# Rows of h_prime by VectorE transposes and DMA hops instead of TensorE, with layer 0 begun three steps sooner

## The chip, the cores and the metric

The kernel runs on one core of a Trainium2 chip. A core has a matrix engine (TensorE, "PE" in the profile), a vector engine (VectorE, "DVE"), an activation engine (ScalarE, "ACT"), a general engine (GpSimd, "POOL") and SyncE ("SP"), which here only issues DMA transfers. Each engine works through its own list of instructions in order; between engines there are semaphores. The metric is the time on the device in microseconds, the median of the runs.

## The reference: what is computed

There are 16 samples, each a graph of 1024 nodes with 128 features and a 1024x1024 adjacency matrix of zeros and ones. Two layers follow one another; each is wrapped in a residual sum and a layer normalization over the features.

```
# layer 0
h = x Ww^T + Wb
e = (h A) h^T;  e = e + e^T
attention = softmax(where(adj > 0, e, 0), axis=1) * adj
h_prime = relu(attention h)
ic = sigmoid(h_prime wi_u + x wi_x)      # one number per node; fc and oc alike
out0 = oc * tanh(ic * h_prime + fc * x)
x = layernorm(x + out0)
# layer 1, four heads
h = x conv_w[hd] + conv_b[hd]
Ah = tanh(adj * (h attn_w[hd] h^T))
Xm = relu(mean over heads of relu(Ah h))
x = layernorm(x + relu(Xm + x))
```

The three gates ic, fc and oc need, for each node, a dot product of its row of h_prime with a vector of 128 weights.

## The kernel before

All is float32. A sample's 1024 nodes are eight blocks of 128 (`NB = 8`), and 1024 columns are two halves of 512 (`NH = 2`).

**The order of work** is written out by hand. The main loop (L602 to L625) goes over samples `b`, and for each over 32 steps of layer 1: four heads times eight blocks `m`. A step (`layer1_step`, L477) is: two score matmuls into PSUM tiles of the tag "sc" (L494), two VectorE products with the adjacency tile (L495), one tanh on ScalarE (L496), and then the `back` of the step two before (`DELAY = 2`), four matmul instructions into `acc` (L500). A float32 matmul of 512 columns shows as two instructions in the profile. On a head's last block `back` also adds the head to the sample's sum on VectorE (L516, L518); with the delay that falls into steps 9, 17, 25 and into step 1 of the next sample. `acc` of layer 1 has a single buffer, so a head's first `back` comes after the sum of the head before. There are four "sc" buffers, used in turn by nearly all PSUM results except the two accumulators.

**Layer 0 of the next sample** is cut into pieces with short names, and the list `BETWEEN` (L592) says which pieces follow which step of layer 1; `AHEAD` (L598) does so for the sample after that. The pieces: L loads xT and the eight adjacency tiles, X loads x; Q and H project; S0 to S7 compute the scores of one row of blocks (upper triangle only); T0 to T6 mirror a row of blocks into the lower triangle; A masks, takes the maximum and exponentiates; B multiplies with the adjacency, scales, and issues the `back` of the block before into `acc0` (L351); R applies relu and leaves h_prime transposed in `hpT` (features in partitions). P and p then bring h_prime into rows: eight TensorE matmuls with `hpT` as the weights against `ident_g` (L370), which is the identity with the three gate vectors as further columns, so the same matmul gives h_prime's rows and its three dot products; ScalarE copies them out (L371). G forms the gates (L377 to L380) and fc * x on GpSimd (L384). I, O, V, N form the inner sum and tanh, the outer sum, the statistics, and the normalized result x1.

**Turning by VectorE and DMA.** `turn` (L220) transposes a 128x1024 tile without TensorE: VectorE transposes each 32x32 block (L224), SyncE writes the tile to DRAM (L226), waits until it has landed, and reads it back by four DMAs with the blocks moved to their places (L229). It is used for x1 (`turn_x1`, after step `TURN`) and for the sum of heads (`layer1_end`, whose four parts come after the steps of `ENDING`); `turn_score` (T, L312 to L319) does the same for the scores. All these DMAs, and the loads, are issued by SyncE, whose queue is in order: while it waits for a write to land, what is behind it waits too.

Layer 0 of sample 0 and the beginning of sample 1's are written out before the loop (L561 to L588), with TensorE doing the transposes of sample 0.

Of the kernel before, what the change touches and what calls it, by code (L numbers as in the profile page):

```python
# [11 lines left out]
F32 = mybir.dt.float32  # L12
AF = mybir.ActivationFunctionType
ALU = mybir.AluOpType
# [3 lines left out]
P = 128  # L18
# [4 lines left out]
def two_layer_adjacency_kernel(  # L23
# [41 lines left out]
    mhalf = consts.tile([P, NB], F32, name="mhalf")  # L65
    nc.gpsimd.memset(mhalf, -0.5)

    a_in = consts.tile([P, P], F32, name="a_in")
    nc.sync.dma_start(a_in, A)
    ww_in = consts.tile([P, P], F32, name="ww_in")  # L70
    nc.sync.dma_start(ww_in, Ww)
    wb_col = consts.tile([P, 1], F32, name="wb_col")
    nc.sync.dma_start(wb_col, Wb.rearrange("(d o) -> d o", o=1))
# [13 lines left out]
    for t, ws in ((gate_x, (wi_x, wf_x, wo_x)), (gate_u, (wi_u, wf_u, wo_u))):  # L87
        for g, w in enumerate(ws):
            nc.scalar.dma_start(t[:, g : g + 1], w.rearrange("(d o) -> d o", o=1))

    def load_late_weights():
        nc.sync.dma_start(cw_in[0:1], conv_b.rearrange("(o h) d -> o h d", o=1))
        nc.sync.dma_start(cw_in[1:P], conv_w[:, 0 : D - 1, :].rearrange("h f d -> f h d"))
        nc.sync.dma_start(cw_last, conv_w[:, D - 1 : D, :].rearrange("h f d -> f h d"))
        nc.sync.dma_start(aw, attn_w.rearrange("h i j -> i h j"))

# [12 lines left out]

    a_sym = consts.tile([P, P], F32, name="a_sym")
    s_ww = consts.tile([P, P], F32, name="s_ww")
    q_w = consts.tile([P, P], F32, name="q_w")
    c_col = consts.tile([P, 1], F32, name="c_col")
    sb_col = consts.tile([P, 1], F32, name="sb_col")
# [101 lines left out]
    def turn(dst, src, name):  # L220


        t = sb.tile([P, N], F32, tag="turn", name=f"turn_{name}", bufs=2)
        nc.vector.transpose(t.rearrange("p (k d) -> p k d", d=P), src)  # L224
        d = dram.tile([P, N], F32, tag="turn", name=f"dram_{name}")
        nc.sync.dma_start(d, t)  # L226
        dv = d.rearrange("(a i) (k c j) -> c i k a j", i=Q, c=P // Q, j=Q)
        for c in range(P // Q):
            nc.sync.dma_start(  # L229
                dst[ts(c, Q)].rearrange("i (k a j) -> i k a j", a=P // Q, j=Q), dv[c]  # L230
            )
# [4 lines left out]
    def layer0(b):  # L236
# [4 lines left out]

        t = {}

        def load():
            t["xT"] = sb.tile([P, N], F32, tag="xT", name=f"xT_{b}")
            nc.sync.dma_start(t["xT"], xT[b])
            adj_t[b] = []
            for j in range(NB):
                a = adjp.tile([P, N], F32, tag="adj", name=f"adj_{b}_{j}")
                nc.sync.dma_start(a, adjT[b, ts(j, P), :])  # L250
                adj_t[b].append(a)

        def load_x():
            t["x"] = sb.tile([P, NB, D], F32, tag="x", name=f"x_{b}", bufs=1)
# [68 lines left out]

        def mask(j):
            s = t["R"][:, :, j, :]
            adj = adj_t[b][j].rearrange("p (k d) -> p k d", d=P)
            for ks in (ts(0, BH), ts(1, BH)) if (b, j) == (0, 0) else [slice(NB)]:
                nc.vector.scalar_tensor_tensor(  # L328
                    s[:, ks], adj[:, ks], 0.0, s[:, ks], op0=ALU.is_gt, op1=ALU.mult
                )  # L330
            nmax = sb.tile([P, 1], F32, tag="nmax", name=f"nmax_{b}_{j}", bufs=4)
            nc.vector.tensor_reduce(nmax, s, AX.XY, ALU.max, negate=True)  # L332
            t["z", j] = sb.tile([P, 1], F32, tag="z", name=f"z_{b}_{j}", bufs=4)
            nc.scalar.activation(s, s, AF.Exp, bias=nmax, accum_out=t["z", j])  # L334

        def weigh(j):

            s = t["R"][:, :, j, :]
            nc.vector.tensor_mul(s, s, adj_t[b][j].rearrange("p (k d) -> p k d", d=P))  # L339
            rz = sb.tile([P, 1], F32, tag="rz", name=f"rz_{b}_{j}", bufs=4)  # L340
            nc.vector.reciprocal(rz, t["z", j])  # L341
            t["hz", j] = sb.tile([P, D], F32, tag="hz", name=f"hz_{b}_{j}", bufs=4)
            nc.scalar.mul(t["hz", j], t["h"][:, j, :D], rz)  # L343
            if j:
                back(j - 1)
# [16 lines left out]
        def rows_hp(groups):  # L362

            if groups[0] is GROUPS[0]:
                t["hp"] = sb.tile([P, NB, D + 3], F32, tag="hp", name=f"hp_{b}", bufs=1)
            for ks in groups:
                pt = small(f"pt0_{b}_{ks[0]}")[:, : len(ks) * (D + 3)]
                pt = pt.rearrange("p (k d) -> p k d", d=D + 3)
                for i, k in enumerate(ks):
                    nc.tensor.matmul(pt[:, i, :], t["hpT"][:, ts(k, P)], ident_g, start=True, stop=True)  # L370
                nc.scalar.copy(t["hp"][:, ks[0] : ks[-1] + 1, :], pt)  # L371

        def gates():

            gate = t["gate"]
            gflat = gate.rearrange("p k g -> p (k g)")
            nc.vector.tensor_add(gate, t["hp"][:, :, D : D + 3], gate)  # L377
            nc.scalar.activation(gflat, gflat, AF.Exp, scale=-1.0)
            nc.vector.tensor_scalar_add(gflat, gflat, 1.0)
            nc.vector.reciprocal(gflat, gflat)  # L380
            t["u"] = sb.tile([P, NB, D], F32, tag="u", name=f"u0_{b}", bufs=1)
            t["x1"] = sb.tile([P, NB, D + 1], F32, tag="x1", name=f"x1_{b}")
            for ks in PARTS:
                nc.gpsimd.tensor_mul(  # L384
                    t["u"][:, ks], t["x"][:, ks],
                    gate[:, ks, 1:2].to_broadcast([P, ks.stop - ks.start, D]),
                )
            nc.gpsimd.memset(t["x1"][:, :, 0:1], 1.0)

        def inner(halves):  # L390
            u, gate, hp = t["u"], t["gate"], t["hp"]
# [19 lines left out]
        def finish(p):  # L411
# [4 lines left out]

        PARTS = [slice(0, NB)] if b else [slice(0, BH), slice(BH, NB)]
        pieces = {
            "L": load, "X": load_x, "R": relu,
            "P": lambda: rows_hp(GROUPS[:-1]), "p": lambda: rows_hp(GROUPS[-1:]),  # L420
            "G": gates,
        }
        for i, ks in enumerate(GROUPS):
            pieces[f"H{i}"] = partial(project_h, [ks])
        for p in range(len(PARTS)):
# [4 lines left out]
        for q in range(NH):  # L430
            pieces[f"Q{q}"] = partial(project_q, q)
        for j in range(NB):
            for name, piece in (("S", score), ("A", mask), ("B", weigh)):
                pieces[f"{name}{j}"] = partial(piece, j)
            if j + 1 < NB:
                pieces[f"T{j}"] = partial(turn_score, j)
        return pieces

    def run(pieces, names):
        for name in names.split():  # L440
            if name in pieces:
                pieces.pop(name)()
# [33 lines left out]

    def layer1_step(b, hd, m):  # L477
        x1T, h1, uT = x1T_t[b], h1_t[b, m], u_t[b, hd]
        adj = adj_t[b][m]
        if m == 0:  # L480
            acc1_t[b, hd] = ps_acc.tile([P, N], F32, tag="acc1", name=f"acc1_{b}_{hd}")
        acc = acc1_t[b, hd]


        last = (b, hd) == (B - 1, H - 1)
        if last:
            if m == 0:
                kept.append(sb.tile([P, NB, N], F32, tag="R", name="kept", bufs=1))
            s = kept[0][:, m, :]
        else:  # L490
            s = sb.tile([P, N], F32, tag="s1", name=f"s1_{b}_{hd}_{m}", bufs=4)
        for q in range(NH):
            ps = ps_sc.tile([P, 512], F32, tag="sc", name=f"sc1_{b}_{hd}_{m}_{q}")
            nc.tensor.matmul(ps, x1T[:, ts(m, P)], uT[:, ts(q, 512)], start=True, stop=True)  # L494
            nc.vector.tensor_mul(s[:, ts(q, 512)], ps, adj[:, ts(q, 512)])  # L495
        nc.scalar.activation(s, s, AF.Tanh)  # L496

        def back(halves=range(NH)):
            for q in halves:
                nc.tensor.matmul(  # L500
                    acc[:, ts(q, 512)], h1[:, ts(hd, D)], s[:, ts(q, 512)],
                    start=(m == 0), stop=(m == NB - 1),
                )
            if m == NB - 1:
                if hd == 0:
                    sum_t[b] = sb.tile([P, N], F32, tag="sum", name=f"sum_{b}", bufs=1)
                for q in halves:
                    add_head(b, hd, acc[:, ts(q, 512)], q * 512)

        push(partial(back, [0]) if last else back)  # L510
# [31 lines left out]
    def last_end(b, k0, k1):  # L542
# [16 lines left out]


    first, second, join = layer0(0), layer0(1), join_weights()  # L561
    run(first, "L X")
    load_late_weights()
    run(second, "L")
    run(first, "Q0 H0 S0 H1 H2 Q1 T0 S1 A0 T1 S2 A1 B0 T2 S3 A2 B1 T3 S4 A3 B2 T4 S5 A4 B3")
    run(first, "T5 S6 A5 B4 T6 S7 A6 B5")
    run(second, "Q0")
    run(first, "A7 B6")
    run(second, "Q1")
    run(first, "B7 R")  # L570
    next(join)
    run(first, "P p G")
    run(second, "H0 H1")
    next(join)
    run(second, "S0")
# [14 lines left out]


    BETWEEN = [  # L592
# [4 lines left out]
    ]  # L597
    AHEAD = {28: "L", 31: "Q0 Q1"}  # L598
    TURN = 27
    ENDING = (DELAY, DELAY + 3, DELAY + 5, DELAY + 7)  # L600
    end, nxt = None, second
    for b in range(B):  # L602
        after = layer0(b + 2) if b + 2 < B else {}
# [72 lines left out]
```

## Time and profile before

Median of 3 runs 2452.89 us (2452.03 to 2454.49). The profiled execution spans 2453.0 us.

| engine | busy us | share |
|---|---|---|
| TensorE, matmuls | 2428.0 | 99% |
| VectorE | 1590.2 | 65% |
| ScalarE | 1082.8 | 44% |
| GpSimd | 112.9 | 5% |

| group | instructions | busy us | mean ns |
|---|---|---|---|
| L370 TensorE, h_prime's rows and gate products | 256 | 33.8 | 275 |
| L371 ScalarE, their copies of 393 and 262 columns | 32 and 16 | 15.6 and 6.0 | 487 and 377 |
| L224 VectorE, block transposes of 128x1024, each of two uses | 15 | 18.5 | 1235 |
| L332 VectorE, a reduction of 128x1024 | 128 | 156.2 | 1220 |
| L384 GpSimd, a product of 128x1024 | 15 | 28.5 | 1898 |

In a line of groups, the first part is line, engine, operation, written and read tiles and shapes; then the count, busy time and mean duration; then the idle time of the engine just ahead of these instructions and what ended it. A line of a timeline is start, duration, engine, line, operation. Matmul instructions overlap in the records (592 ns each, while one starts every 429 ns), so TensorE's pace is read from starts.

### The profile page before, as it was taken

To read this page: it belongs to the slowest core of one execution; us is meant where nothing else is said; L and a number is where in the kernel's file an instruction comes from. 1 tells how busy PE (TensorE), PEld (TensorE's weight loads), DVE (VectorE), ACT (ScalarE), POOL (GpSimd) and SP (SyncE) were. 2 spreads that over 40 slices of the span, in tenths; PEclk is the share of its full clock that TensorE was granted. 3 is DMA by queue.
4 is the path that set the end of the run, shared out by engine and by line. 5 is a ranking of instruction groups with operands and counts; after the bars stand their busy time and mean duration, and the time that the engine had idled before them with its cause. 6 is when DMAs were issued, how large, how long until landed. Compare 5 with 4: busy or idle time off the path is not lost.

```text
span 2453.0 us, 19886 instructions
## 1 busy us (share of the span) xinstructions
PE 2428.0 (99%) x6175; PEld 1121.2 (46%) x6175; DVE 1590.2 (65%) x3017; ACT 1082.8 (44%) x1522; POOL 112.9 (5%) x94
## 2 busy tenths in 40 slices
PE   8999999999999999999999999999999999999998
PEld 4444444444444444444444444444444444444444
DVE  6665847657476575865658666585765857658454
ACT  5444444444444444434444444444444444444432
POOL 0000000000000000000000000000000000000000
PEclk9999999999999999999999999999999999999999
DMA  4204223041240512405123140332404223042010
GB/s 174 58 11 133 56 94 86 9 145 44 95 95 3 152 35 94 95 15 147 27 104 85 41 129 20 119 70 76 102 12 130 60 94 84 11 135 55 17 26 9
DMA packets 409056, 180.76 MB, mean 74 GB/s; under 512 B 352630, under 2 KB 377078, under 8 KB 408951
## 3 DMA queue, kind: packets, MB, share of 16 engines
q1 hardware_dynamic: 405927, 171.63, 25.1%
q0 software_dynamic: 2160, 7.87, 1.1%
q8 instruction: 49, 0.80, 0.1%
q14 instruction: 56, 0.46, 0.1%
q10 hardware_dynamic: 864, 0.00, 0.0%
HBM read 127.80 MB, written 51.64 MB: 73 GB/s over the span
## 4 chain that ended last, share of the span: by engine, by line
PE 92%; DVE 3%; DMA 2%; SPq 1%; POOL 0%; issue 0%; ACT 0%; POOLq 0%; DVEq 0%; ACTq 0%
PE sc L494 33%; PE acc L500 33%; PE acc L351 9%; PE sc L287 5%; PE pT_u L200 4%; PE pR L465 4%; DMA xT<-in_xT_dram 2%; PE pT_q L200 1%; PE pt L370 1%; PE pR_h L271 1%; SPq L229 1%; DMA dram_x<-turn_x 1%; DVE x L191 0%; DVE st L183 0%; POOL rs L188 0%
## 5 line engine op out<-in xcount | busy, mean ns | idle before, releaser
L495 DVE TENSOR_TENSOR s<-sc,adj 128x512 f32<-128x512 f32 x1008 | 671.3, 685 | 625.6 <-PE sc L494 613.8
L494 PE MATMUL sc<-uT,x1T 128*128 128x512 f32 x2048 | 962.0, 592 | 0.0
L500 PE MATMUL acc<-s,h 128*128 128x512 f32 x2016 | 947.4, 592 | 0.0
L496 ACT ACTIVATE s<-s 128x1024 f32<-128x1024 f32 x504 | 532.9, 1057 | 806.0 <-DVE s L495 799.6
L500 PEld LDWEIGHTS acc<-s,h 128*128 128x128 f32 x2016 | 381.7, 190 | 483.7 <-issue 474.4
L494 PEld LDWEIGHTS sc<-uT,x1T 128*128 128x128 f32 x2048 | 385.7, 190 | 468.8 <-issue 421.9
L351 PE MATMUL acc<-R,hz 128*128 128x512 f32 x512 | 241.2, 594 | 4.8 <-ACT hz L343 4.8
L334 ACT ACTIVATE R<-R,nmax 128x1024 f32<-128x1024 f32 x128 | 147.0, 1148 | 210.4 <-DVE nmax L332 182.4
L339 DVE TENSOR_TENSOR R<-R,adj 128x1024 f32<-128x1024 f32 x128 | 156.2, 1220 | 5.4 <-ACT R L334 0.2
L332 DVE TENSOR_REDUCE nmax<-R 128x1 f32<-128x1024 f32 x128 | 156.2, 1220 | 4.4
L328 DVE SCALAR_TENSOR_TENSOR R<-adj,R 128x1024 f32<-128x1024 f32 (+1 forms) x129 | 153.2, 1188 | 1.4 <-PE turn L305 1.4
L351 PEld LDWEIGHTS acc<-R,hz 128*128 128x128 f32 x512 | 95.6, 190 | 111.7 <-issue 85.6
L287 PE MATMUL sc<-xT,qT 128*128 128x512 f32 (+3 forms) x384 | 145.8, 489 | 0.5 <-ACT R L290 0.5
L290 ACT ACTIVATE R<-sc,h 128x512 f32<-128x512 f32 (+1 forms) x192 | 109.0, 578 | 38.5 <-PE sc L287 37.1
L188 POOL TENSOR_TENSOR rs<-rs,mhalf 128x8 f32<-128x8 f32 (+2 forms) x35 | 65.8, 1880 | 1212.4 <-DVE rs L187 886.7
L200 PE MATMUL pT_u<-x1T,ms 128*128 128x512 f32 x256 | 120.4, 592 | 0.0
L465 PE MATMUL pR<-cw,x1T 128*128 128x512 f32 x256 | 114.9, 592 | 0.0
L343 ACT ACTIVATE hz<-h,rz 128x128 f32<-128x128 f32 x128 | 51.2, 400 | 126.1 <-DVE rz L341 126.0
L287 PEld LDWEIGHTS sc<-xT,qT 128*128 128x128 f32 x384 | 70.0, 191 | 70.4 <-issue 57.1
L468 ACT COPY h<-pR 128x512 f32<-128x512 f32 x128 | 74.9, 585 | 41.9 <-PE pR L465 41.9
L312 DVE STREAM_TRANSPOSE turn<-R 128x896 f32<-128x896 f32 (+6 forms) x105 | 73.3, 699 | 16.1 <-DMA dram<-turn 14.9
L518 DVE SCALAR_TENSOR_TENSOR sum<-acc,sum 128x512 f32<-128x512 f32 x95 | 61.3, 686 | 33.7 <-PE acc L500 32.9
(104 smaller groups left out, 957.4 us busy)
## 6 DMA issues: line engine op xcount, KB each, us to landing
adj<-in_adjT_dram SPq DMA_DIRECT2D x128, 512.0 KB, 8.2
xT<-in_xT_dram SPq DMA_DIRECT2D x16, 512.0 KB, 4.9
x<-in_x_dram SPq DMA_DIRECT2D x16, 512.0 KB, 4.1
dram_x<-turn_x SPq DMA_DIRECT2D x15, 512.0 KB, 2.6
x1T<-dram_x SPq DMA_DIRECT2D x60, 128.0 KB, 3.2
dram_sum<-turn_sum SPq DMA_DIRECT2D x15, 512.0 KB, 2.6
y<-dram_sum SPq DMA_DIRECT2D x60, 128.0 KB, 3.3
out_dram<-y POOLq DMA_DIRECT2D x15, 512.0 KB, 4.0
```

The costliest lines, as they stand in the source:

```text
L200: nc.tensor.matmul(ps, w, src[:, ts(q, 512)], start=True, stop=True)
L287: nc.tensor.matmul(ps[:, : at - lo], t["qT"][:, ts(j, P)], t["xT"][:, lo:at], start=True, stop=True)
L328: nc.vector.scalar_tensor_tensor(s[:, ks], adj[:, ks], 0.0, s[:, ks], op0=ALU.is_gt, op1=ALU.mult)
L332: nc.vector.tensor_reduce(nmax, s, AX.XY, ALU.max, negate=True)
L334: nc.scalar.activation(s, s, AF.Exp, bias=nmax, accum_out=t["z", j])
L339: nc.vector.tensor_mul(s, s, adj_t[b][j].rearrange("p (k d) -> p k d", d=P))
L351: nc.tensor.matmul(t["acc"][:, ts(q, 512)], t["hz", j], t["R"][:, ts(q, BH), j, :], start=(j == 0), stop=(j == NB - 1),)
L465: nc.tensor.matmul(ps, x1T_t[b][:, ts(k, P)], cw.rearrange("p h d -> p (h d)"), start=True, stop=True)
L494: nc.tensor.matmul(ps, x1T[:, ts(m, P)], uT[:, ts(q, 512)], start=True, stop=True)
L495: nc.vector.tensor_mul(s[:, ts(q, 512)], ps, adj[:, ts(q, 512)])
L496: nc.scalar.activation(s, s, AF.Tanh)
L500: nc.tensor.matmul(acc[:, ts(q, 512)], h1[:, ts(hd, D)], s[:, ts(q, 512)], start=(m == 0), stop=(m == NB - 1),)
```

## The change

For samples 1 to 15, h_prime's rows no longer come from TensorE. P is now a `turn` of `hpT` (VectorE block transposes, a DRAM write, four DMA hops). The gates' dot products are formed from the rows: Y multiplies, on GpSimd, the rows with each weight vector, which is kept broadcast over the partitions in `wu_b`; F, i and o sum the products over the features by VectorE reductions, add the part that comes from x, and take the sigmoid. F does the forget gate alone and then fc * x; i and o do the other two. The products take the two buffers of the tag "turn", which T, `turn` and `hpT` use as well. Sample 0 keeps the old way.

From relu to the inner sum there are now more steps (P, Y, an empty one, F, i, o), and layer 0 of the next sample begins three steps sooner: Q, H, S0, T0 and S1 move to the steps 28 to 31 of the sample before, and what follows moves up by three steps. The adjacency tiles are loaded one by one (L0 to L7), each after the step that frees its buffer, and xT (now W) at step 20. x1 is turned after step 28 instead of 27, and the parts of `layer1_end` come after steps 2, 4, 6, 8 instead of 2, 5, 7, 9. Four weight tiles of the start share the buffers of `hz`, to make room.

```diff
@@ load_late_weights @@
+        for g, w in enumerate((wi_u, wf_u, wo_u)):
+            nc.sync.dma_start(wu_b[:, g, :], w.partition_broadcast(P))
@@ layer0 @@
-        def load():
+        def load_xT():
             t["xT"] = sb.tile([P, N], F32, tag="xT", name=f"xT_{b}")
             nc.sync.dma_start(t["xT"], xT[b])
-            adj_t[b] = []
-            for j in range(NB):
-                a = adjp.tile([P, N], F32, tag="adj", name=f"adj_{b}_{j}")
-                nc.sync.dma_start(a, adjT[b, ts(j, P), :])
-                adj_t[b].append(a)
+
+        def load_adj(j):
+            a = adj_t[b, j] = adjp.tile([P, N], F32, tag="adj", name=f"adj_{b}_{j}")
+            nc.sync.dma_start(a, adjT[b, ts(j, P), :])
...
+        def turn_hp():
+            t["hp"] = sb.tile([P, NB, D], F32, tag="hp", name=f"hp_{b}", bufs=1)
+            hpT = t["hpT"].rearrange("p (k d) -> p k d", d=P)
+            turn(t["hp"].rearrange("p k d -> p (k d)"), hpT, f"hp_{b}")
+
+        def weigh_hp():
+
+            for g in (1, 0, 2):
+                t["hw", g] = sb.tile([P, NB, D], F32, tag="turn", name=f"hw_{b}_{g}", bufs=2)
+                nc.gpsimd.tensor_mul(
+                    t["hw", g], t["hp"], wu_b[:, g : g + 1, :].to_broadcast([P, NB, D])
+                )
+
+        def sum_hp(g):
+            hw = sb.tile([P, NB, 1], F32, tag="hw", name=f"hws_{b}_{g}")
+            nc.vector.tensor_reduce(hw, t["hw", g], AX.X, ALU.add)
+            gate = t["gate"][:, :, g : g + 1]
+            nc.vector.tensor_add(gate, hw, gate)
...
+        def gate_f():
+            sum_hp(1)
+            sigmoid(t["gate"][:, :, 1:2])
+            forget()
+
+        def gate_i():
+            sum_hp(0)
+
+        def gates_io():
+            sum_hp(2)
+            sigmoid(t["gate"][:, :, 0:3:2])
...
-            "P": lambda: rows_hp(GROUPS[:-1]), "p": lambda: rows_hp(GROUPS[-1:]),
-            "G": gates,
+            "W": load_xT, "X": load_x, "R": relu,
         }
+        if b == 0:
+            pieces.update(P=lambda: rows_hp(GROUPS), G=gates)
+        else:
+            pieces.update(P=turn_hp, Y=weigh_hp, F=gate_f, i=gate_i, o=gates_io)
...
-    run(first, "Q0 H0 S0 H1 H2 Q1 T0 S1 A0 T1 S2 A1 B0 T2 S3 A2 B1 T3 S4 A3 B2 T4 S5 A4 B3")
+    run(first, "Q0 H0 S0 Q1 T0 S1 A0 H1 H2 T1 S2 A1 B0 T2 S3 A2 B1 T3 S4 A3 B2 T4 S5 A4 B3")
...
     BETWEEN = [
-        "H0 H1 H2", "S0", "T0 S1", "T1 S2", "T2 A0", "S3 B0", "T3 A1", "S4 B1",
-        "T4 A2", "S5 B2", "T5 A3", "S6 B3", "T6 A4", "S7 B4", "A5", "B5",
-        "A6", "B6", "A7", "B7", "X R", "P", "p G", "I0",
-        "O0", "V0", "N0", "", "", "", "", "",
+        "L7 T1 S2", "T2 A0", "S3 B0", "T3 A1", "S4 B1", "T4 A2", "S5 B2", "T5 A3",
+        "S6 B3", "T6 A4", "S7 B4", "A5", "B5", "A6", "B6", "A7",
+        "B7", "X R", "P", "Y", "", "F", "i", "o",
+        "I0", "O0", "V0", "N0", "", "", "", "",
     ]
-    AHEAD = {28: "L", 31: "Q0 Q1"}
-    TURN = 27
-    ENDING = (DELAY, DELAY + 3, DELAY + 5, DELAY + 7)
+    AHEAD = {
+        20: "W", 25: "L0", 26: "L1", 27: "L2", 28: "L3 Q0 Q1", 29: "L4 H0 H1 H2",
+        30: "L5 S0", 31: "L6 T0 S1",
+    }
+    TURN = 28
+    ENDING = (DELAY, DELAY + 2, DELAY + 4, DELAY + 6)
```

More of the change, by code (lines that the diff above doesn't have):

```diff
@@ L66, in two_layer_adjacency_kernel @@
     nc.gpsimd.memset(mhalf, -0.5)
-    a_in = consts.tile([P, P], F32, name="a_in")
+    a_in = sb.tile([P, P], F32, tag="hz", name="a_in", bufs=4)
     nc.sync.dma_start(a_in, A)
-    ww_in = consts.tile([P, P], F32, name="ww_in")
+    ww_in = sb.tile([P, P], F32, tag="hz", name="ww_in", bufs=4)
     nc.sync.dma_start(ww_in, Ww)
@@ L89, in two_layer_adjacency_kernel @@
             nc.scalar.dma_start(t[:, g : g + 1], w.rearrange("(d o) -> d o", o=1))
+    wu_b = consts.tile([P, 3, D], F32, name="wu_b")
     def load_late_weights():
@@ L110, in two_layer_adjacency_kernel @@
     ms = consts.tile([P, H, P], F32, name="ms")
-    a_sym = consts.tile([P, P], F32, name="a_sym")
-    s_ww = consts.tile([P, P], F32, name="s_ww")
+    a_sym = sb.tile([P, P], F32, tag="hz", name="a_sym", bufs=4)
+    s_ww = sb.tile([P, P], F32, tag="hz", name="s_ww", bufs=4)
     q_w = consts.tile([P, P], F32, name="q_w")
@@ L325, in mask @@
             s = t["R"][:, :, j, :]
-            adj = adj_t[b][j].rearrange("p (k d) -> p k d", d=P)
+            adj = adj_t[b, j].rearrange("p (k d) -> p k d", d=P)
             for ks in (ts(0, BH), ts(1, BH)) if (b, j) == (0, 0) else [slice(NB)]:
@@ L338, in weigh @@
             s = t["R"][:, :, j, :]
-            nc.vector.tensor_mul(s, s, adj_t[b][j].rearrange("p (k d) -> p k d", d=P))
+            nc.vector.tensor_mul(s, s, adj_t[b, j].rearrange("p (k d) -> p k d", d=P))
             rz = sb.tile([P, 1], F32, tag="rz", name=f"rz_{b}_{j}", bufs=4)
@@ L371, in rows_hp, with sigmoid, forget @@
                 nc.scalar.copy(t["hp"][:, ks[0] : ks[-1] + 1, :], pt)
[L373 to L380, printed above, removed]
+        def turn_hp():
[13 more added lines that the diff above has]
+            nc.vector.tensor_add(gate, hw, gate)
+        def sigmoid(gate):
+            nc.scalar.activation(gate, gate, AF.Exp, scale=-1.0)
+            nc.vector.tensor_scalar_add(gate, gate, 1.0)
+            nc.vector.reciprocal(gate, gate)
+        def forget():
             t["u"] = sb.tile([P, NB, D], F32, tag="u", name=f"u0_{b}", bufs=1)
@@ L385, in gates @@
                     t["u"][:, ks], t["x"][:, ks],
-                    gate[:, ks, 1:2].to_broadcast([P, ks.stop - ks.start, D]),
+                    t["gate"][:, ks, 1:2].to_broadcast([P, ks.stop - ks.start, D]),
                 )
             nc.gpsimd.memset(t["x1"][:, :, 0:1], 1.0)
+        def gates():
+            gate = t["gate"]
+            nc.vector.tensor_add(gate, t["hp"][:, :, D : D + 3], gate)
+            sigmoid(gate.rearrange("p k g -> p (k g)"))
+            forget()
+        def gate_f():
+            sum_hp(1)
+            sigmoid(t["gate"][:, :, 1:2])
+            forget()
+        def gate_i():
[3 more added lines that the diff above has]
+            sigmoid(t["gate"][:, :, 0:3:2])
         def inner(halves):
@@ L418, in layer0 @@
         pieces = {
-            "L": load, "X": load_x, "R": relu,
-            "P": lambda: rows_hp(GROUPS[:-1]), "p": lambda: rows_hp(GROUPS[-1:]),
-            "G": gates,
-        }
+            "W": load_xT, "X": load_x, "R": relu,
+        }
+        if b == 0:
+            pieces.update(P=lambda: rows_hp(GROUPS), G=gates)
+        else:
+            pieces.update(P=turn_hp, Y=weigh_hp, F=gate_f, i=gate_i, o=gates_io)
         for i, ks in enumerate(GROUPS):
@@ L432, in layer0 @@
         for j in range(NB):
-            for name, piece in (("S", score), ("A", mask), ("B", weigh)):
+            for name, piece in (("L", load_adj), ("S", score), ("A", mask), ("B", weigh)):
                 pieces[f"{name}{j}"] = partial(piece, j)
@@ L478, in layer1_step @@
         x1T, h1, uT = x1T_t[b], h1_t[b, m], u_t[b, hd]
-        adj = adj_t[b][m]
+        adj = adj_t[b, m]
         if m == 0:
@@ L561, in two_layer_adjacency_kernel @@
     first, second, join = layer0(0), layer0(1), join_weights()
-    run(first, "L X")
+    run(first, "W L0 L1 L2 L3 L4 L5 L6 L7 X")
     load_late_weights()
-    run(second, "L")
-    run(first, "Q0 H0 S0 H1 H2 Q1 T0 S1 A0 T1 S2 A1 B0 T2 S3 A2 B1 T3 S4 A3 B2 T4 S5 A4 B3")
+    run(second, "W L0 L1 L2 L3 L4 L5 L6 L7")
+    run(first, "Q0 H0 S0 Q1 T0 S1 A0 H1 H2 T1 S2 A1 B0 T2 S3 A2 B1 T3 S4 A3 B2 T4 S5 A4 B3")
     run(first, "T5 S6 A5 B4 T6 S7 A6 B5")
@@ L571, in two_layer_adjacency_kernel @@
     next(join)
-    run(first, "P p G")
+    run(first, "P G")
     run(second, "H0 H1")
```

## The prediction

> **What bounds the kernel now.** I read the busy shares first, then the chain of work that ended last.
>
> ```profile
> PE 2428.0 (99%) x6175; PEld 1121.2 (46%) x6175; DVE 1590.2 (65%) x3017; ACT 1082.8 (44%) x1522; POOL 112.9 (5%) x94
> ...
> PE 92%; DVE 3%; DMA 2%; SPq 1%; POOL 0%; issue 0%; ACT 0%; POOLq 0%; DVEq 0%; ACTq 0%
> ```
>
> TensorE sets the time. Since matmul ends are modelled, I check that with starts. In the timeline four matmul instructions of 512 columns start every 1.716 us (503.13 to 504.85 and so on). Per sample there are 324 such instructions (128 of L494, 128 of L500, 32 of L351, 16 of L200 for uT, 16 of L465, 4 of L200 for qT): 139.0 us. L287 adds 4608 columns a sample, 7.7; L271 1.80; L370 1.79. Sum 150.3 us. The chain gives the period, from one L271 to the next:
>
> ```profile
> 368.36 1.80 PE pR_h L271 x16
> ...
> 519.37 1.80 PE pR_h L271 x16
> ...
> 669.80 1.80 PE pR_h L271 x16
> ```
>
> 151.01, then 150.43 us. The undisturbed period is the bare sum of TensorE's work. The excess is this wait, at the border between two samples:
>
> ```profile
> 503.13 1.88 PE L500 MATMUL acc<-s,h 128*128 128x512 f32 x4
> 505.40 1.96 PE L200 MATMUL pT_q<-xT,q_w 128*128 128x512 f32 x4 [0.39 <-DMA xT<-in_xT_dram]
> ```
>
> 505.40 - 504.85 = 0.55 us lost. Over the 14 borders that I can measure this way the periods exceed 150.38 by 6.4 us, and the first border (204.00 instead of 203.37) loses 0.6: 7.0 us in all. The wait table's 4.5 us counts from the modelled end.
>
> The second thing to see is VectorE around the last head's sum, since a step's place in VectorE's order decides what it delays (step 1 starts at 521.01 on TensorE):
>
> ```profile
> 522.93 0.69 DVE L495 TENSOR_TENSOR s<-sc,adj 128x512 f32<-128x512 f32 x1 [0.17 <-PE sc L494]
> 524.64 1.29 DVE L518 SCALAR_TENSOR_TENSOR sum<-acc,sum 128x512 f32<-128x512 f32 x2 [1.02 <-PE acc L500]
> ```
>
> The sum can't begin before the step's own acc matmuls end, so VectorE isn't free before 4.85 us into a step of 3.43.
>
> **What the Trainium skill says.** "SBUF — State Buffer", "Who interferes with whom": a VectorE instruction with two SBUF inputs waits for a GpSimd instruction that reads SBUF; a reduction never does. The trace agrees: L394 takes 347 ns in the median but at most 1117, and the eight of it at 54.8, beside the second product of L384, take 2.96 us instead of 2.2. L495 (one input in PSUM) isn't held: 627 to 694 ns always. "VectorE: DVE Perf Modes", "The three transpose paths": VectorE transposes only 32x32 blocks; so the blocks have to be moved by DMA, as L226 and L229 do. "DMA: Bandwidth & Descriptors", "Two DMAs through the same engine are not ordered": the hop out of DRAM has to wait for the write's completion. In the trace SyncE waits in L319 for its write 105 times, 229.6 us in all, and everything behind it in its queue waits too.
>
> **The change part by part.** Removed for 15 of 16 samples: L370 on TensorE.
>
> ```profile
> 465.30 1.88 PE L494 MATMUL sc<-uT,x1T 128*128 128x512 f32 x4
> ...
> 468.73 1.50 PE L370 MATMUL pt<-ident_g,hpT 128*128 128x131 f32 x12
> ...
> 470.07 1.88 PE L494 MATMUL sc<-uT,x1T 128*128 128x512 f32 x4
> ...
> 473.50 0.61 PE L370 MATMUL pt<-ident_g,hpT 128*128 128x131 f32 x4
> ...
> 473.95 1.88 PE L494 MATMUL sc<-uT,x1T 128*128 128x512 f32 x4
> ```
>
> 468.73 to 470.07 is 1.34, 473.50 to 473.95 is 0.45: 1.79 us a sample, x15 = 26.9 us, all on the path. ScalarE's three copies (1.35 us a sample) go too; it was at 44%.
>
> xT is now loaded at step 20 and used at step 28, 30 us later; it took 4.9 us to land. The border's wait goes: 7.0 us. The adjacency tiles come one at a time, each a step after its buffer's last reader; needed at step 1 at the earliest: nothing.
>
> The start: Q1 and T0 no longer stand behind H1 and H2 (1.15 us of TensorE at 13.87), VectorE's first mask begins about that much sooner, but H1's and H2's adds come back later in a stretch where VectorE is the chain (19 to 45). I take 0.7 us of the possible 0 to 1.1. The extra weight rows delay the second xT by some 1.5 us; it lands at about 34 and is wanted at 40: nothing.
>
> h_prime's rows: transpose 1.24 us (L224), write and four hops. For x1T the first issue is at 494.40 and the last hop lands at about 502.6, 8.2 us. hpT is ready before step 18's products end, so rows are there at 2.4 + 1.3 + 8.2 = 11.9 us after step 18 starts. GpSimd's product: 1.90 each by L384 (128x1024, same form), so the first is done at 13.9. VectorE reaches F after step 21's products: steps 18 to 20 last 3 x 3.43 + 1.72 = 12.0, plus 2.5 = 14.5. No wait, with 0.6 us to spare; I allow 0 to 2. The three reductions cost 1.22 each (L332), but the small adds have two SBUF inputs and can each be held by a product, up to 1.9. VectorE does 4.7 us more in steps 21 to 23 (three reductions and six small operations of 0.18), and these have little else; by my count it enters step 25 no later than before (its place then: 483.11, 2.3 after TensorE's). That matters, because acc of the next head waits at step 26 for the sum of step 25 with 0.1 to 0.2 us in hand (485.73 to 485.97). I put it at 0, with 1 us a sample as the far end.
>
> x1T's turn is a step later, but steps 28 to 31 now hold Q, H, S0 and S1 (6.7 us of TensorE): it lands some 15 us into step 28 and is needed at 20. Nothing.
>
> **Where time is given back.** Layer 0 three steps sooner puts T2 and A0 into step 1, the step of the sum. VectorE: 4.85, then T2 0.77, A0 2.36 (1.22 + 1.14, 543 less 540.57), so step 2's first product starts at 7.98 and ends at 8.67. TensorE: step 1 is 3.43, step 2 with S3 4.51, so step 3 would start at 7.94. There are four score buffers, and step 2 uses four (two products, two of S3): step 3's first matmul needs the buffer of step 2's first product. Wait 8.67 + 0.1 - 7.94 = 0.8; with the 0.15 of restart that the xT wait shows, 0.95 us. Before, A0 stood in step 4, without a sum, with 1.72 us of uT behind it.
>
> A second new wait: the sum's turn is read two steps later, not three. On SyncE a turn takes 6 us:
>
> ```profile
> 529.95 0.33 SPq L226 DMA_DIRECT2D dram_sum<-turn_sum  x1
> 532.69 3.64 SPq L229 DMA_DIRECT2D y<-dram_sum  x4
> 536.43 0.62 SPq L316 DMA_DIRECT2D dram<-turn  x1
> ```
>
> T2 is now ahead of it in that queue: T2 written at 5.65, its hops issued by 11.5, the sum's rows landed at 11.5 + 8.8 = 20.3. VectorE wants them in step 4 at 16.9 and is held 3.4 us, with steps 5 to 9 behind it. From there it is busy without a gap (21.9 us by the rows of L495, L536, L339, L328, L332, L183, L191) to step 9's sum at 42.2; its first half is done at 42.9, and TensorE wants it at 43.3. So it just fits: 0, at most 2 if the hops land 2 us later. I take 0.05. It concerns the samples with a predecessor and a successor, 14: 14 x 1.0 = 14 us.
>
> Sum: 2452.9 - 26.9 - 7.0 - 0.7 + 14 = 2432.3.
>
> **The rivals.** (a) All is hidden: 2452.9 - 34.6 = 2418.3. For it: VectorE at 65%, products of before up to 3.3 us late without loss. Against: the buffer count above. (b) VectorE's lateness costs a further 1 us a sample, by the sum's rows, or by adds held by products until the acc of step 26 is late: 2432.3 + 14 = 2446. For it: 0.4 and 0.2 us in hand. Against: the products run while VectorE mostly has PSUM operands. (c) The end on the other side, slower: each of the three reductions waits a whole product (rows late, or products slowed by VectorE): 5.7 us of VectorE standing still, of which some 2.8 is covered by the buffers, so 2.9 x 15 = 43.5: 2462. For it: GpSimd was idle 95% and nothing of before shows four products in a row. Against: the one product there takes 1.90 beside a busy VectorE each time.
>
> **How the numbers follow.** Forecast 0.52, (a) 0.22, (b) 0.17, (c) 0.09. Time 2432. Range: from just under (a), 2416, to just over (b), 2449; it leaves out (c) and the outer edges. Faster by over 0.2% means below 2448: 0.52 + 0.22 + 0.14 = 0.88; within: 0.03 of (b) and 0.02 of (c), 0.05; slower: 0.07.
>
> **What would show it.** TensorE's period near 149.5 us (148.6 in case a); no pt matmuls after the first sample; no wait of pT_q on xT; one gap of about 0.9 us a sample ahead of step 3's sc, released by VectorE; VectorE waiting some 3 us for the hops of the sum's rows ahead of the residual sum (now L536); the first reduction of h_prime waiting under 1 us for GpSimd. It is wrong if the period stays above 150, if acc of a head's first step waits for the sum, or if the border waits for x1T.

## The result, and the profile after

The changed kernel takes 2464.01 us (median of 4 runs, 2460.73 to 2465.90), against 2453.24: a ratio of 1.0042, interval 1.0025 to 1.006. It is slower, by 0.4%; the forecast was 2432.

The first parts of the page of after, busy shares and chain:

```profile
PE 2411.8 (98%) x5935; PEld 1093.0 (44%) x5935; DVE 1696.6 (69%) x3137; ACT 1065.1 (43%) x1492; POOL 218.4 (9%) x139
...
PE 70%; DVE 14%; DMA 9%; SPq 3%; issue 2%; POOL 1%; ACT 1%; POOLq 0%; DVEq 0%; ACTq 0%
```

TensorE has 240 instructions less, and the chain, which was TensorE's to 92%, now leaves it for VectorE, DMA and SyncE over a quarter of the span: there are new waits. (In the fences below, `...` marks lines left out.) From the chain, in order of time, one sample's start to the next one's:

```profile
1262.47 1.80 PE pR_h L275 x16
1413.15 1.80 PE pR_h L275 x16
1564.59 1.80 PE pR_h L275 x16
```

150.68 and 151.44 us; the bare sum of TensorE's work is now 148.6. What is missing can be read from starts: four matmul instructions of 512 columns take 1.716 us, and where the next one starts later, that is lost. In the changed kernel there are three such places in a sample, the same ones in each. One sample of TensorE's timeline (the sample with the longest wait of step 6) shows all three, at steps 3, 6 and 26:

```profile
532.76 1.24 PE L291 MATMUL sc<-xT,qT 128*128 128x128 f32 x4
534.58 1.98 PE L536 MATMUL sc<-uT,x1T 128*128 128x512 f32 x4 [0.58 <-DVE s L537]
...
547.56 1.88 PE L542 MATMUL acc<-s,h 128*128 128x512 f32 x4
552.39 3.27 PE L536 MATMUL sc<-uT,x1T 128*128 128x512 f32 x4 [2.95 <-DVE s L537]
```

```profile
639.61 1.88 PE L536 MATMUL sc<-uT,x1T 128*128 128x512 f32 x4
643.24 1.96 PE L542 MATMUL acc<-s,h 128*128 128x512 f32 x4 [1.76 <-DVE sum L560]
```

| TensorE's time lost, us in all | before | after |
|---|---|---|
| border of samples, pT_q waits for xT | 6.0 | 0 |
| step 3, sc waits for a score buffer | 0 | 10.3 (14 x 0.74) |
| step 6, sc | 0 | 15.6 (14, from 0.1 to 4.5) |
| step 26, acc waits for the sum | 0 | 14.5 (15, from 0.5 to 1.9) |
| the next start after a wait at steps 3 and 6, 0.10 late each time | 0 | 2.8 |

The 4.5 us at step 6 belong to the sample shown. TensorE stood there for 3.0 us, and from 552.9 to 556.3 the profile shows a granted clock of 0.5: the matmuls start 0.85 us apart instead of 0.43, which is 1.3 us of the 4.5.

The gains came as forecast: rows -26.9, xT -6.0, the start -0.5 (layer 1's first matmul at 73.58, before at 74.10). The new waits are 43.2, and some 2 us more lie in the start after each wait of step 26 (0.07) and in one wait for x1T. Together 2453.0 - 33.4 + 45 = 2464.6; the profiled span is 2464.1.

**What stands behind step 6.** VectorE's timeline of the same sample, from the products of step 4 on:

```profile
541.54 1.28 DVE L537 TENSOR_TENSOR s<-sc,adj 128x512 f32<-128x512 f32 x2
548.05 1.22 DVE L578 SCALAR_TENSOR_TENSOR y<-y,x 128x1024 f32<-128x1024 f32 x1 [5.24 <-DMA y<-dram_sum]
...
551.59 0.16 DVE L345 RECIPROCAL rz<-z 128x1 f32<-128x1 f32 x1
```

VectorE stands for 5.24 us (the longest; 46.8 over 15 samples, 3.1 each) until the rows of the sum of heads are back. SyncE's queue says why they are late:

```profile
531.60 0.33 SPq L320 DMA_DIRECT2D dram<-turn  x1
533.80 2.63 SPq L323 DMA_DIRECT2D R<-dram  x4
536.53 0.58 SPq L231 DMA_DIRECT2D dram_sum<-turn_sum  x1
542.31 3.37 SPq L234 DMA_DIRECT2D y<-dram_sum  x4
```

The sum's write is issued only when T2's hops are (536.43), and here it lands in 5.6 us (3.3 in the median, 2.6 before). The products of step 5 stand behind the rows in VectorE's order, so they come late too. How this reaches TensorE is seen in three instructions, each shown alone: step 5's first product, the first copy of uT on ScalarE, and step 6's first matmul:

```profile
551.66 0.67 DVE L537 TENSOR_TENSOR s<-sc,adj 128x512 f32<-128x512 f32 x1
552.09 0.56 ACT L207 COPY uT<-pT_u 128x512 f32<-128x512 f32 x1
552.39 0.71 PE L536 MATMUL sc<-uT,x1T 128*128 128x512 f32 x1 [2.95 <-DVE s L537]
```

The matmul takes the score buffer that this product empties: in all 14 samples it starts 0.05 to 0.06 us after the product's end. The buffers are thus not used strictly in turn, as was said of the kernel before. In turn, this matmul would take the buffer of the first copy of uT, but it starts 0.26 us before that copy ends, again in all 14.

The copies are late too, for a related reason. ScalarE works in order, and ahead of them stands `hz` of B1, which needs a reciprocal that VectorE computes after the rows:

```profile
551.78 0.40 ACT L347 ACTIVATE hz<-h,rz 128x128 f32<-128x128 f32 x1 [7.24 <-DVE rz L345]
```

The weight load of step 6's second tile does wait for a copy, 14 times, but no further start is lost by it: this tile comes 0.10 us late, as after the wait of step 3, where there is no copy.

**What stands behind step 26.** VectorE in step 21, and GpSimd's products beside it:

```profile
624.36 0.69 DVE L537 TENSOR_TENSOR s<-sc,adj 128x512 f32<-128x512 f32 x1 [0.17 <-PE sc L536]
626.86 1.22 DVE L392 TENSOR_REDUCE hws<-hw 128x8 f32<-128x1024 f32 x1 [1.81 <-POOL hw L386]
628.11 1.05 DVE L394 TENSOR_TENSOR gate<-hws,gate 128x8 f32<-128x8 f32 x1
629.44 2.02 DVE L399 TENSOR_SCALAR gate<-gate 128x8 f32<-128x8 f32 x1 [0.28 <-ACT gate L398]
631.50 0.20 DVE L400 RECIPROCAL gate<-gate 128x8 f32<-128x8 f32 x1
631.62 1.24 DVE L537 TENSOR_TENSOR s<-sc,adj 128x512 f32<-128x512 f32 x2
```

```profile
624.47 6.96 POOL L386 TENSOR_TENSOR hw<-hp,wu_b 128x1024 f32<-128x1024 f32 x3 [54.66 <-DMA xT<-in_xT_dram]
```

The addition and the tensor_scalar of 8 elements take 1.05 and 2.02 us, 0.17 and 0.18 where no product runs: each ends when a product does (629.17 and 631.43). Step 22's products start 4.7 us after they could. In step 25 VectorE is still 2 us behind: it comes 4.4 us after TensorE, before the change 2.3. The sum of heads follows there, and step 26's acc (643.24) waits for its end:

```profile
640.61 1.29 DVE L537 TENSOR_TENSOR s<-sc,adj 128x512 f32<-128x512 f32 x2
641.81 1.28 DVE L560 SCALAR_TENSOR_TENSOR sum<-acc,sum 128x512 f32<-128x512 f32 x2
```

### The profile page after: what moved, and what is told of

The parts are those of the page before. It is cut to its first block, busy times and chain, and to the rows that moved or that the text cites. A ratio compares the mean times of both kernels' runs of the same rounds, so it can differ in the third digit from the quotient of the medians.

```text
span 2464.1 us, 19610 instructions
## 1 busy us (share of the span) xinstructions
PE 2411.8 (98%) x5935; PEld 1093.0 (44%) x5935; DVE 1696.6 (69%) x3137; ACT 1065.1 (43%) x1492; POOL 218.4 (9%) x139
## 4 chain that ended last, share of the span: by engine, by line
PE 70%; DVE 14%; DMA 9%; SPq 3%; issue 2%; POOL 1%; ACT 1%; POOLq 0%; DVEq 0%; ACTq 0%
PE sc L536 24%; PE acc L542 24%; PE acc L355 8%; PE pR L507 4%; PE sc L291 4%; DVE s L537 3%; PE pT_u L205 3%; DMA hp<-dram_hp 2%; SPq L234 2%; DMA y<-dram_sum 2%; DVE hws L392 2%; DMA dram_sum<-turn_sum 2%; DMA dram_hp<-turn_hp 1%; DVE u L434 1%; POOL hw L386 1%
## 5 line engine op out<-in xcount | busy, mean ns | idle before, releaser
L537 DVE TENSOR_TENSOR s<-sc,adj 128x512 f32<-128x512 f32 x1008 | 664.6, 683 | 560.1 <-PE sc L536 555.4
L542 PE MATMUL acc<-s,h 128*128 128x512 f32 x2016 | 948.9, 593 | 12.2 <-DVE sum L560 12.2
L386 POOL TENSOR_TENSOR hw<-hp,wu_b 128x1024 f32<-128x1024 f32 x45 | 104.5, 2346 | 842.8 <-DMA hp<-dram_hp 788.1
L207 ACT COPY uT<-pT_u 128x512 f32<-128x512 f32 x128 | 73.2, 583 | 55.3 <-PE pT_u L205 55.3
```

What stands on the lines that cost most here:

```text
L542: nc.tensor.matmul(acc[:, ts(q, 512)], h1[:, ts(hd, D)], s[:, ts(q, 512)], start=(m == 0), stop=(m == NB - 1),)
```

## The experiments

Each is the changed kernel with the edit shown, save e6. All ratios are to the kernel before, run beside it on the same chip. The changed kernel's own ratio is known to 0.0018 either way, some 4 us, so a difference to it of 2 or 3 us says nothing by its time alone.

**e1, the rows of the sum read one step later.**

```diff
-    ENDING = (DELAY, DELAY + 2, DELAY + 4, DELAY + 6)
+    ENDING = (DELAY, DELAY + 3, DELAY + 4, DELAY + 6)
```

> The changed kernel with one edit: the parts of layer1_end after steps 2, 5, 6, 8, so the rows of the sum of heads are read one step later. Theory (three separate waits): the wait of step 6's score matmul, 14.4 us over 14 samples in the changed kernel, goes; the other two stay (step 3: 10.3, step 26: 14.5). 2464 - 14 = 2450, between 2448 and 2453. Rival (VectorE is simply loaded too much, lateness only moves on): less than half comes back, 2457 to 2464. Second rival (the small DMA packets of the new hops slow the whole): nothing comes back, 2462 to 2466.

Measured 2447.72 us, ratio 0.9977 (0.9967 to 0.9987): 16.3 us under the changed kernel. That is just below the expected range. TensorE's starts: step 6 loses nothing, step 3 still 10.4 and step 26 still 13.9. One wait is gone, the others stay: the theory. This one digit alone turns the change into a gain.

**e2, A0 out of the sum's step.**

```diff
-        "L7 T1 S2", "T2 A0", "S3 B0", "T3 A1", "S4 B1", "T4 A2", "S5 B2", "T5 A3",
+        "L7 T1 S2", "T2 S3", "A0", "T3 B0 A1", "S4 B1", "T4 A2", "S5 B2", "T5 A3",
```

> The changed kernel with one edit: S3 moves from step 2 to step 1, A0 from step 1 to step 2, B0 from step 2 to step 3. Theory: the wait of step 3's score matmul for a score buffer (0.74 x 14 = 10.3 us) goes, the wait of step 6 for the rows of the sum stays or grows by up to 0.3 a sample, because VectorE's order up to step 4 is as full as before: 2454 to 2458. Rival (lateness only moves on): all of it comes back at step 6, 2462 to 2465.

Measured 2461.82, ratio 1.0038 (1.0025 to 1.0051): 2.2 us under the changed kernel, which is not clear of the noise. Step 3's wait is gone in every sample (10.3 us), but step 6 now loses 23.9 us instead of 15.6. My theory missed here, and the rival was right: TensorE comes earlier to a place where it waits for a time set by the DMA. The first of two waits in a row is worth little until the second is gone.

**e3, one sigmoid for the three gates.**

```diff
         def gate_f():
             sum_hp(1)
-            sigmoid(t["gate"][:, :, 1:2])
-            forget()
...
         def gates_io():
             sum_hp(2)
-            sigmoid(t["gate"][:, :, 0:3:2])
+            nc.vector.tensor_add(t["gate"], t["hws"], t["gate"])
+            sigmoid(t["gate"].rearrange("p k g -> p (k g)"))
+            forget()
```

(`sum_hp` only reduces, into one column of `hws`.)

> The changed kernel with one edit: F and i only reduce, and the addition, the sigmoid of all three gates and the product fc * x come together after the third reduction at step 23. Then no VectorE instruction with two SBUF inputs, and no tensor_scalar from SBUF, meets a running GpSimd product. Theory: the tensor_scalar of 2.02 us and the addition of 1.05 us fall to 0.18 each, the first reduction's wait for GpSimd (12.9 us in all) stays, and the wait of step 26's acc for the sum falls from 14.5 us to under 3: 2451 to 2454. Rival (the reductions themselves and the late rows are the lateness, not the held small operations): the wait of step 26 keeps more than half, 2456 to 2462.

Measured 2449.14, ratio 0.9984 (0.9975 to 0.9992): 14.9 us under the changed kernel, 2 us better than expected. VectorE in steps 21 to 23 of e3:

```profile
621.38 1.22 DVE L393 TENSOR_REDUCE hws<-hw 128x8 f32<-128x1024 f32 x1 [1.02 <-POOL hw L386]
622.52 1.28 DVE L536 TENSOR_TENSOR s<-sc,adj 128x512 f32<-128x512 f32 x2
623.71 1.21 DVE L393 TENSOR_REDUCE hws<-hw 128x8 f32<-128x1024 f32 x1
...
627.14 1.21 DVE L393 TENSOR_REDUCE hws<-hw 128x8 f32<-128x1024 f32 x1
628.39 0.18 DVE L425 TENSOR_TENSOR gate<-hws,gate 128x24 f32<-128x24 f32 x1
628.86 0.18 DVE L398 TENSOR_SCALAR gate<-gate 128x24 f32<-128x24 f32 x1 [0.29 <-ACT gate L397]
```

The first reduction still waits for GpSimd (13.2 us in all), and step 26 loses nothing. What was left out is the meeting of the small operations with the products.

**e5, two of the three products left out** (the gates ic and oc are then computed with the wrong weights; every VectorE instruction stays).

```diff
-            for g in (1, 0, 2):
+            for g in (1,):
...
+            t["hw", 0] = t["hw", 2] = t["hw", 1]
```

> The changed kernel with two of the three GpSimd products left out: all three reductions read the first product, so the gates ic and oc use the wrong weights; every VectorE instruction stays. Theory (VectorE's small operations are held by the GpSimd products that run beside them): the tensor_scalar of F falls from 2.02 to about 0.18 us, the addition too, and step 26's acc waits for the sum under 4 us in all instead of 14.5: 2450 to 2454. Rival (the late rows and the three reductions are the lateness): step 26 keeps over 8 us, 2457 to 2464.

Measured 2448.70, ratio 0.9983 (0.9976 to 0.999): 15.3 us under the changed kernel, somewhat more than expected. The same instruction of F, in the same place, with no product beside it:

```profile
L400 DVE TENSOR_SCALAR gate<-gate 128x8 f32<-128x8 f32 x15 | 2.6, 174 | 4.2 <-ACT gate L399 4.2
```

174 ns instead of 2024, and step 26 loses nothing. e3 changed VectorE's order, e5 only GpSimd's work; both give the same. The first reduction's wait for the rows stays in both (12.2 us here), and by itself it costs no time at step 26.

**e6, the kernel before with xT at step 20 alone.**

```diff
-    AHEAD = {28: "L", 31: "Q0 Q1"}
+    AHEAD = {20: "W", 28: "L", 31: "Q0 Q1"}
```

(W loads xT, L the adjacency.)

> The kernel before with one part of the change alone: xT is loaded at step 20, the adjacency as before at step 28. Theory: the border's wait of pT_q on xT goes, 6.3 us by the starts of TensorE in the profile of before: 2452.7 - 6.3 = 2446.4, ratio 0.9974. Rival (the wait only moves, to x1T or to the adjacency tiles): ratio 0.999 to 1.001.

Measured 2448.02, ratio 0.9977 (0.9969 to 0.9985): 4.9 us less, the expected 6.3 within the interval. No wait is left at the border.

**e7, T2 behind the sum's turn.**

```diff
-        "L7 T1 S2", "T2 A0", "S3 B0", "T3 A1",
+        "L7 T1 S2", "A0", "T2 S3 B0", "T3 A1",
```

> The changed kernel with one edit: T2 goes from step 1 to step 2, behind the sum's turn, so that in SyncE's queue the sum's write stands ahead of T2's write and hops, and step 1 has 0.77 us less of VectorE. Theory (the sum's rows are late because T2's turn holds SyncE's queue): VectorE's wait for the rows falls from 3.1 us a sample to under 1.5, step 6's wait goes, and step 3's wait (0.74) goes as step 2's first product starts 0.77 us sooner: 2464 - 14 - 10 = 2440, between 2437 and 2446. Rival (the rows are late because write and hops themselves take that long): the wait for the rows stays over 2.5 us and step 6 keeps or raises its wait: 2452 to 2462.

Measured 2436.71, ratio 0.9938 (0.9925 to 0.9951): 27.3 us under the changed kernel, just under what was expected. SyncE's queue in e7:

```profile
531.67 0.33 SPq L231 DMA_DIRECT2D dram_sum<-turn_sum  x1
535.07 2.74 SPq L234 DMA_DIRECT2D y<-dram_sum  x4
537.91 0.91 SPq L320 DMA_DIRECT2D dram<-turn  x1
```

The write goes out as soon as VectorE has turned the sum, and VectorE's wait for the rows falls from 46.8 to 18.4 us in all. Steps 3 and 6 lose almost nothing (1.7 and 0.8 us); 16 us remain, those of step 26. So the order in SyncE's queue made the rows late.

**e8, the uT projection ahead of the layer-0 pieces of its step.**

```diff
+            if hd < H - 1 and m == NB - 4:
+                head_uT(b, hd + 1)
             run(nxt, BETWEEN[step])
...
-            elif hd < H - 1 and m == NB - 4:
-                head_uT(b, hd + 1)
```

> The changed kernel with one edit: the projection uT of the next head is issued ahead of the layer-0 pieces of its step, so that at step 4 ScalarE's two copies of uT stand ahead of hz of B1, which waits for VectorE. Theory (step 6's score matmul waits for a buffer that the uT copies free late, because ScalarE's queue stands at hz while VectorE waits for the rows of the sum): step 6's wait falls from 14.4 us to under 3 although VectorE waits for the rows as long as before (3 us a sample): 2450 to 2454. Rival (it is VectorE's own lateness, the buffer of step 5's product): step 6 keeps over half, 2457 to 2464.

Measured 2450.02, ratio 0.9988 (0.9979 to 0.9996): 14.0 us under the changed kernel. VectorE waits for the rows as before, 44.3 us in all, and step 6 loses nothing. ScalarE in e8:

```profile
540.72 1.06 ACT L207 COPY uT<-pT_u 128x512 f32<-128x512 f32 x2
541.66 0.70 ACT L294 ACTIVATE R<-sc,h 128x512 f32<-128x512 f32 x1
548.58 0.40 ACT L347 ACTIVATE hz<-h,rz 128x128 f32<-128x128 f32 x1 [6.22 <-DVE rz L345]
```

`hz` still waits 6.22 us, but the copies are already done. The time is the one that the theory gave, and yet this doesn't show that the copies were the cause, because the edit changed something else too. Step 5's first product on VectorE and step 6's matmuls in e8:

```profile
548.46 1.27 DVE L537 TENSOR_TENSOR s<-sc,adj 128x512 f32<-128x512 f32 x2
546.12 1.88 PE L536 MATMUL sc<-uT,x1T 128*128 128x512 f32 x4
```

Step 6 now starts before that product has even begun, and in all 14 samples before it has ended (0.2 to 3.0 us). It can't be taking the product's buffer any more: with the projection issued sooner, the buffers fall to other tiles. So e8 shows that VectorE's standing reaches step 6 through a score buffer. It doesn't separate the buffer of step 5's product (the rival) from those of the copies, since it frees step 6 of both. For the changed kernel the starts above decide: it is the product, and that the theory's time came true was luck. Had the product been in time, the copies would have held step 6's second tile for up to 2.5 us in the sample shown, by an estimate from the times there (the first copy ends at 552.65, and the tile was due 0.86 us after 549.28); no run shows that alone.

**e4, the edits of e1, e2 and e3 together.**

> The three edits together. Theory: 2464 - 10.3 - 14.4 - 12 = 2427, between 2422 and 2433, with TensorE's period at 148.6 to 149.1 us. Rival (lateness moves on): not under 2440.

Measured 2421.25, ratio 0.9869 (0.9855 to 0.9882). The chain of e4:

```profile
1086.97 1.80 PE pR_h L275 x16
1235.61 1.80 PE pR_h L275 x16
1384.25 1.80 PE pR_h L275 x16
```

A period of 148.64 us, which is the bare sum of TensorE's work. With e1 and e3 alone one would reckon 2464.0 - 16.3 - 14.9 = 2432.8; by that reckoning the third edit, worth 2.2 us by itself, is worth 11.6 here, about the 10.3 of step 3's wait. (e1 and e3 without e2 were not run.) Against e6, which keeps the rows on TensorE and loses nothing at the border either, e4 is 26.8 us faster: within the noise of some 3 us, 15 samples x 1.79 us, the worth of the rows alone.

**e9, the edits of e7 and e3 together.**

> The changed kernel with two edits: T2 behind the sum's turn (step 2), and one sigmoid for the three gates after the third reduction. Theory (each wait has its own cause, and these two edits take away all three): 2436.7 - 14.5 = 2422, between 2419 and 2425, the same as with the three edits. Rival (the two share VectorE's lateness): over 2427.

Measured 2422.95, ratio 0.9884 (0.9868 to 0.9901). Two edits do nearly what three did: both kernels are faster than the one before, by 1.2 and 1.3%, and than the changed one.

## Why the prediction was wrong, point by point

**The bound: right.** TensorE's work, taken from starts, gave the period of before, and 148.6 us as the floor, which e4 reaches.

**What is removed: right.** 26.9 us for the rows (e4 against e6: 26.8). xT: 7.0 predicted, 6.0 by the starts (6.8 with the slower start after each wait), 4.9 by e6, whose interval reaches from 3.7 to 7.6. The start 0.7, measured 0.5.

**Step 3's wait: right in mechanism, 0.95 predicted, 0.84 measured.** That is 0.74 and 0.10 for the restart, where the prediction had 0.8 and 0.15. e2 takes it away, e7 all but the 0.10.

**The rows of the sum: the step that failed first.** "So it just fits: 0, at most 2" - it was 1.1 us a sample. VectorE's wait itself was about right (3.4 predicted, 3.1 measured on average), and so was its cause, T2's turn ahead in SyncE's queue (e7). I had "steps 5 to 9 behind it", and then followed this lateness only as far as step 9's sum, where it "just fits". The products of the steps between also empty score buffers, and I left out the check that I had made for step 3 just above: when does TensorE need the buffer that the late product empties? At step 6 it needs the one of step 5's first product, and has to wait, whether or not step 9's sum is in time. That step 6 starts 0.05 to 0.06 us after that product in every sample shows this wait; e1 and e7, in which VectorE stands for the rows not at all or for 1.2 us on average, take it away.

**The gates: the step that failed second.** "I put it at 0, with 1 us a sample as the far end" - it was the far end, 0.97. I named the additions with two SBUF inputs as what a product can hold, and left out the tensor_scalar, which has one and was held longest, 1.85 us every time. The section that I cited, "Who interferes with whom" of "SBUF — State Buffer" in the Trainium skill, does name it: a tensor_scalar can enter a mode with two ports, and then contends with GpSimd. The trace agrees that it is held: 2024 ns beside products, 174 without (e5). That it was in this mode no run shows. The reductions, which the page says are never held, took 1205 to 1221 ns always. The products cost 2.35 us each and not 1.90, and the rows landed some 14 instead of 12 us after step 18 began. In e3 both are still there and step 26 loses nothing, so neither costs anything by itself.

**The addition of the parts.** The forecast gave back 14 us, the trace shows 45. Rival (b) had both of these mechanisms, but 1 us a sample for the two together, where each took that. Rival (c) had nearly the time, 2462, by luck, for another reason: no reduction waited for a whole product (0.9 us on average for the first, the others not at all). The range was drawn from the two as alternatives; since they have different causes (e4 and e9), they should have been summed.

## What to carry to other kernels

Where an engine is late, list every buffer that it then empties late, not only the result at the end of its work, and look up where the bound engine takes that buffer next: here the products of one step, 3.1 us late on average, cost 15.6 us. Waits in a row hide one another, so undoing the first shows nothing clear (e2: 2 us) until the later one is gone (by reckoning 12 us); test edits together as well as alone. An edit that moves an instruction can also change who gets which buffer, so that a time which comes out as the theory says (e8) doesn't prove the theory: compare in the trace what each instruction's start follows. An operation moved to an idle engine isn't free for its neighbour: put the neighbour's small operations where no product runs.

## What the runs showed of the hardware that I had not expected

A tensor_scalar of 8 elements with one SBUF input was held by a running GpSimd product until its end (2.02 us instead of 0.17), just as the addition of 8 elements with two inputs was (1.05 instead of 0.17): both ended 0.03 us after the product, in all 15 samples. A GpSimd product of 128x1024 took 2.35 us where the second operand was a row of 128 repeated over the blocks (in e5 too, where VectorE had nothing that was held), and 1.90 us where it was one number per block repeated over the row. A write of 512 KB to DRAM, which landed in 2.6 us with the queue empty (e7), took up to 5.6 when it was issued behind the hops of another turn. After TensorE's longest wait at step 6, the granted clock was 0.5 for 3.4 us, in the changed kernel and at the same step of e3 and e5. In e2 it stayed at 1 after a wait there of 2.6 us, longer than that of e3 (2.2 us), so the length of one wait alone doesn't decide it.
